# The newest queries' fetch moved ahead of the key store in a cross-attention kernel

## The chip, the cores and the metric

The kernel runs on one NeuronCore of a Trainium2 chip. The metric is the time of one execution in device microseconds. A core has a matrix engine (TensorE, "PE" in the profile), a vector engine (VectorE, "DVE"), a scalar engine (ScalarE, "ACT"), a general engine (GpSimd, "POOL") and SyncE ("SP"), which here does nothing but start transfers (DMAs). The engines run side by side. Each goes through its own list of instructions in order and stops where an instruction has to wait for another engine or for a transfer.

## What is computed

For each of 64 batch elements: 256 text rows of 512 numbers (x) and 256 audio rows of 384 numbers (the context), all in float32.

```
text_p  = x   @ W_text  + b_text        # queries before their layer norm
audio_p = ctx @ W_audio + b_audio       # keys before their layer norm; also the values
Q = layer_norm(text_p, g1, beta1)
K = layer_norm(audio_p, g2, beta2)
alpha = softmax(Q @ K.T / sqrt(512))
y = (alpha @ audio_p) @ W_out + b_out
out = layer_norm(y + x, g_out, beta_out)
```

## The kernel before

**What a batch element goes through.** TensorE contracts over the partition dimension, so what a product contracts over has to lie along the partitions. Rows come out of a projection with the hidden dimension along the free axis, but the scores need it along the partitions. The kernel turns them by way of DRAM. The normalised rows of the queries (`qr`) and of the keys (`kr`) are stored to a scratch tensor in DRAM (`qd`, `kd`; `Projection.store`, L425, one transfer of 512 KB) and fetched again as blocks of 32 by 32 (`qq`, `kq`; `Projection.fetch`, which calls `squares`, L88, four transfers of 128 KB). VectorE then transposes each block of 32 by 32 in place (`turn`: L91 for the queries, L446 for the keys), and ScalarE applies gain and shift per hidden column (`affine`, L453). The exponentials take the same way (`store_e` L556, `fetch_e`, tiles `ed` and `eq`), and x and the context are fetched as squares from the inputs (`load_x`, `load_c`, tiles `xq` and `cq`), and once more as plain rows (`load_x_rows` L112, `load_c_rows` L116).

**Products.** Each projection (queries, keys, output) is one matrix product of two by two blocks, written with seven block products instead of eight (`Blocks.products`, L482); VectorE adds them out of the accumulator banks into the rows (`Blocks.leave`, L494). Six banks (`p_pj`) serve all three projections in turn. Two more (`p_at`) take scores and context.

**Rounds.** The order on each engine is written out by hand. The main loop runs over b = 0 to 61. Round b does, in this order:

1. scores of element b, then the rest of the output of element b − 2; the squares of x and context of b + 3 are turned; row maxima and exponentials of b;
2. the query products of b + 2, between them the division of the exponentials;
3. SyncE: fetch of the queries and the keys of b + 1, store of the exponentials of b, load of context squares and x squares of b + 4, fetch of the exponentials of b, x rows of b, context rows of b + 1;
4. turn and affine of the queries of b + 1 (VectorE, ScalarE); context product of b − 1; turn and affine of the keys of b + 1; the output of b − 2 is settled and stored;
5. normalisation (`normalise`, L415) and store of the queries of b + 2;
6. the key products of b + 2, their evictions, normalisation and store;
7. most of the output products of b − 1.

So on SyncE's queue, in order, one round reads: q fetch (b + 1), k fetch (b + 1), e store, context squares, x squares, e fetch, x rows, context rows, output store, q store (b + 2), k store (b + 2). A fetch waits until its store has landed. A store waits until its rows are ready. All these transfers go through one hardware queue onto the core's 16 transfer engines.

The first round fetches nothing in step 3 (its own queries and keys are fetched ahead of the loop). Rounds 60 and 61 load no further squares. After the loop the last two elements are written out by hand; that part begins with the fetch of the queries and keys of element 63. Buffers: the squares `qq` and `kq` have two each, the scratch tensors `qd` and `kd` three each.

Of the kernel before, what the change touches and what calls it, by code (L numbers as in the profile page):

```python
# [22 lines left out]
def kernel(  # L23
# [43 lines left out]
    B, L, D = x.shape  # L67
# [28 lines left out]
    def load_c(b):  # L96
        cq = blk.tile([P, S // SQ, DA // NQ], F32, tag="cq", name=f"cq_{b}")
        squares(cq, c[b])
        blocks[b] = [cq]

    def load_x(b):
        xq = blk.tile([P, L // SQ, D // NQ], F32, tag="xq", name=f"xq_{b}")
        squares(xq, x[b])
        blocks[b].append(xq)
# [5 lines left out]
    def load_x_rows(b):  # L110
        x_rows[b] = xin.tile([P, LT, D], F32, tag="x", name=f"x_{b}")
        nc.sync.dma_start(x_rows[b], x[b].rearrange("(t p) d -> p t d", p=P))  # L112

    def load_c_rows(b):
        c_rows[b] = cin.tile([P, ST, DA], F32, tag="c", name=f"c_{b}")
        nc.sync.dma_start(c_rows[b], c[b].rearrange("(t p) d -> p t d", p=P))  # L116
# [16 lines left out]
    def row(v, name):  # L133
        t = const.tile([P, H], F32, tag=name, name=name)
        nc.sync.dma_start(t, v.rearrange("(o h) -> o h", o=1).broadcast_to([P, H]))
        return t
# [621 lines left out]
    def turn_next(b):  # L758
        xT[b] = turn_x(b)
        xs[b] = sum_x(xT.pop(b))  # L760
        cT[b] = turn_c(b)
        cs[b] = sum_c(cT.pop(b))
# [7 lines left out]
    q, k, xT, cT = {}, {}, {}, {}  # L770
# [111 lines left out]
    for b in range(B - 2):  # L882
        three = b + 3 < B
        at = Attention(b)
        at.scores()
        if done:
            done.o.leave(3, 4)
            done.o.leave(7)
            done.add_x()
        if three and b:  # L890
            turn_next(b + 3)
        if last:
            last.turn_e()
        at.maxima()
        at.exponentials()
        if not b:
            k[1].turn()
        q2 = q[b + 2] = Blocks("q", b + 2, xs.pop(b + 2), wt_blocks, bt_sb)
        q2.products(*((1, 6) if b else (1, 2, 6)))
        q2.leave(1)  # L900
        q2.leave(6)
        at.reciprocals()
        at.divide_e()
        if not b:
            k[1].affine(g2_sb, be2_sb)
        if b:
            q[b + 1].fetch()
            k[b + 1].fetch()
        at.store_e()
        if b + 4 < B:  # L910
            load_c(b + 4)
        if not b:
            at.fetch_e()
        if b + 4 < B:
            load_x(b + 4)
        if b:
            at.fetch_e()
            load_x_rows(b)
        if not three:
            load_x_rows(b + 1)  # L920
        load_c_rows(b + 1)
        if b == 1:
            go_sb = row(g_out, "go")
            beo_sb = row(beta_out, "beo")
        if done:
            done.statistics()
        q2.products(*((2, 5) if b else (5,)))
        q2.leave(2, 5)
        q2.products(3, 4)
        q2.leave(3, 4)  # L930
        q2.products(7)
        q2.leave(7)
        q2.square()
        q2.scales()
        q[b + 1].turn()
        if not b:
            turn_next(3)
        if done:
            done.shift(0)
            done.shift(1)  # L940
        if last:
            last.context()
        q[b + 1].affine(g1_sb, be1_sb)
        if b:
            k[b + 1].turn()
            k[b + 1].affine(g2_sb, be2_sb)
        if done:
            done.settle(0)
            done.settle(1)
            done.store()  # L950
        q2.normalise()
        q2.store()
        if last:
            last.start_products()
        k2 = k[b + 2] = Blocks("k", b + 2, cs.pop(b + 2), wa_blocks, ba_sb)
        k2.products(1, 6)
        k2.leave(1)
        k2.leave(6)
        k2.products(2, 5)
        k2.leave(2, 5)  # L960
        k2.products(3, 4)
        k2.leave(3, 4)
        k2.products(7)
        k2.leave(7)
        k2.square()
        k2.scales()
        k2.normalise()
        k2.store()
        if last:
            last.o.products(1, 6)  # L970
            last.o.leave(1)
            last.o.leave(6)
            last.o.products(2, 5)
            last.o.leave(2, 5)
            last.o.products(3, 4)
            last.o.products(7)
        done, last = last, at


    at = Attention(B - 2)  # L980
    q[B - 1].fetch()
    k[B - 1].fetch()
    load_x_rows(B - 1)
    load_c_rows(B - 1)
# [105 lines left out]
```

## Time and profile before

| | us |
|---|---|
| time, median of 3 runs | 1415.64 (1413.58 to 1415.87) |
| the profiled execution, whole | 1416.99 |
| its span | 1415.2 |
| TensorE busy | 1404.5 |
| VectorE busy | 1229.0 |
| ScalarE busy | 935.1 |
| GpSimd busy | 870.6 |
| share of the 16 transfer engines' time on the main queue | 80.0% |

The profile comes from one execution; the times come from runs of their own. A busy line such as "1404.5 (99%) x6437" gives busy time, share of the span and number of instructions. In a list of waits each line gives who waited at which line for whom, the total in us, how often, and the longest. A line of the view in order of time gives start and duration in us, engine, source line, operation, tile written and tile read; transfers are shown on SyncE's queue ("SPq") with the time that issuing them took, not the time they travelled. The page gives the latter separately as the median from issue to landing:

```profile
kq<-kd SPq DMA_DIRECT2D x256, 128.0 KB, 3.4
qd<-qr SPq DMA_DIRECT2D x64, 512.0 KB, 4.8
qq<-qd SPq DMA_DIRECT2D x256, 128.0 KB, 3.3
```

SyncE's own waits, the largest of them:

```profile
SPq L425 <- ACT kr L415: 197.0, 62, 3.2
SPq L425 <- DVE kr L494: 93.5, 61, 1.9
SPq L425 <- ACT qr L415: 68.4, 59, 1.4
SPq L556 <- ACT e L552: 68.0, 57, 1.4
...
SPq L88 <- DMA kd<-kr: 19.2, 58, 1.0
SPq L88 <- DMA qd<-qr: 17.1, 18, 4.6
```

### The profile page before, as it was taken

What the parts mean: (1) busy time and instruction counts of PE and PEld (TensorE: products, weight loads), DVE (VectorE), ACT (ScalarE), POOL (GpSimd) and SP (SyncE); (2) the same over time, 40 slices, a digit from 0 to 9 for tenths busy, and PEclk for the clock granted to TensorE, in tenths of its full rate; (3) what the DMA queues carried; (4) which work ended last, traced back from release to release, by engine and by line L of the source; (5) the groups of instructions that cost most, each with busy time, mean ns of one, the idle gap of its engine ahead of it and who ended that gap; (6) DMA issues with size and microseconds to landing.
All of it is one profiled execution on the core that took longest, in us unless ns stands there. A gap on an engine that the chain in (4) does not pass through costs nothing.

```text
span 1415.2 us, 22762 instructions
## 1 busy us (share of the span) xinstructions
PE 1404.5 (99%) x6437; PEld 1219.7 (86%) x6437; DVE 1229.0 (87%) x1757; ACT 935.1 (66%) x2298; POOL 870.6 (62%) x1294
## 2 busy tenths in 40 slices
PE   9999999999999999999999999999999999999998
PEld 5788888888888888888888888888888888888885
DVE  5789888988988988988889889889888898898887
ACT  4667676676676676766766766767667667667663
POOL 5557656656666666566566666665665665666645
PEclk9999999999999999999999999999999999999999
DMA  7898887887888787887887887877888788788864
GB/s 198 212 249 245 243 238 220 240 241 221 234 232 229 232 228 236 234 226 237 229 233 232 220 241 233 227 238 228 226 242 239 221 236 239 222 235 226 229 199 125
DMA packets 450579, 322.58 MB, mean 228 GB/s; under 512 B 154900, under 2 KB 382996, under 8 KB 450452
## 3 DMA queue, kind: packets, MB, share of 16 engines
q1 hardware_dynamic: 450356, 320.98, 80.0%
q8 instruction: 52, 0.85, 0.3%
q14 instruction: 75, 0.61, 0.1%
q10 hardware_dynamic: 96, 0.13, 0.0%
HBM read 204.09 MB, written 116.92 MB: 227 GB/s over the span
## 4 chain that ended last, share of the span: by engine, by line
PE 94%; DMA 3%; DVE 1%; POOL 1%; SPq 1%; ACT 0%; issue 0%; DVEq 0%; ACTq 0%
PE ps_q L482 26%; PE ps_k L482 20%; PE ps_y L482 20%; PE ps_sc L521 15%; PE ps_z L587 12%; DMA qd<-qr 1%; PE ps_y L634 1%; DMA ba<-in_L_xattn_b_audio_dram 1%; DMA qq<-qd 0%; DMA xq<-in_x_dram 0%; DMA bt<-in_L_xattn_b_text_dram 0%; SPq L88 0%; DMA c<-in_ctx_dram 0%; DVE qr L494 0%; DMA kd<-kr 0%
## 5 line engine op out<-in xcount | busy, mean ns | idle before, releaser
L494 DVE TENSOR_TENSOR qr<-ps_q,qr 128x512 f32<-128x512 f32 x252 | 174.3, 692 | 88.3 <-PE ps_q L482 85.3
L521 PE MATMUL ps_sc<-kT,qT 128*128 128x256 f32 x1024 | 231.7, 379 | 1.1 <-ACT qT L453 1.1
L348 POOL TENSOR_SCALAR ve<-var 128x2 f32<-128x2 f32 x126 | 43.1, 342 | 290.3 <-ACT junk L387 290.1
L521 PEld LDWEIGHTS ps_sc<-kT,qT 128*128 128x128 f32 x1024 | 194.2, 190 | 28.8 <-ACT qT L453 2.1
L538 ACT ACTIVATE e<-ps_sc,nmx 128x256 f32<-128x256 f32 x128 | 59.4, 469 | 228.7 <-DVE nmx L531 228.7
L603 POOL TENSOR_TENSOR yr<-yr,x 128x512 f32<-128x512 f32 x124 | 155.6, 1277 | 70.2 <-DVE yr L494 70.2
L482 PE MATMUL ps_q<-wtsum,xsum 128*128 128x256 f32 x756 | 193.8, 379 | 0.2 <-POOL xsum L312 0.2
L494 DVE TENSOR_TENSOR kr<-ps_k,kr 128x512 f32<-128x512 f32 x252 | 174.3, 692 | 22.1 <-DVE kr L494 0.5
L494 DVE TENSOR_TENSOR yr<-ps_y,yr 128x512 f32<-128x512 f32 x248 | 171.5, 692 | 21.8 <-DVE yr L494 0.5
L482 PE MATMUL ps_k<-wa,cT 128*128 128x256 f32 x630 | 177.1, 379 | 0.0
L587 PE MATMUL ps_z<-eT,c 128*128 128x256 f32 x768 | 176.2, 379 | 0.0
L482 PE MATMUL ps_y<-wao,zT 128*128 128x256 f32 x620 | 174.1, 379 | 0.0
L350 POOL TENSOR_TENSOR rstd<-ve,nhalf 128x2 f32<-128x2 f32 x192 | 157.1, 818 | 16.0
L587 PEld LDWEIGHTS ps_z<-eT,c 128*128 128x128 f32 x768 | 145.9, 190 | 20.3 <-issue 0.5
L482 PEld LDWEIGHTS ps_q<-wtsum,xsum 128*128 128x128 f32 x756 | 143.6, 190 | 20.0 <-POOL xsum L312 0.6
L453 ACT ACTIVATE qT<-qT,columns 128x256 f32<-128x256 f32 x256 | 132.9, 591 | 8.0 <-DVE qT L91 8.0
L482 PEld LDWEIGHTS ps_k<-wa,cT 128*128 128x128 f32 x630 | 119.6, 190 | 16.2
L453 ACT ACTIVATE kT<-kT,columns 128x256 f32<-128x256 f32 x256 | 132.0, 586 | 1.4 <-DVE kT L446 1.0
L415 ACT ACTIVATE kr<-kr,rstd 128x512 f32<-128x512 f32 x126 | 84.0, 714 | 72.3 <-POOL rstd L350 72.3
L482 PEld LDWEIGHTS ps_y<-wao,zT 128*128 128x128 f32 x620 | 117.7, 190 | 16.0
L387 ACT ACTIVATE junk<-kr 128x512 f32<-128x512 f32 x126 | 79.4, 630 | 77.5 <-DVE kr L494 73.1
L482 PE MATMUL ps_q<-wt,xT 128*128 128x256 f32 x504 | 129.1, 379 | 0.0
(159 smaller groups left out, 2973.0 us busy)
## 6 DMA issues: line engine op xcount, KB each, us to landing
kd<-kr SPq DMA_DIRECT2D x64, 512.0 KB, 3.1
kq<-kd SPq DMA_DIRECT2D x256, 128.0 KB, 3.4
qd<-qr SPq DMA_DIRECT2D x64, 512.0 KB, 4.8
qq<-qd SPq DMA_DIRECT2D x256, 128.0 KB, 3.3
xq<-in_x_dram SPq DMA_DIRECT2D x252, 128.0 KB, 2.8
x<-in_x_dram SPq DMA_DIRECT2D x63, 512.0 KB, 4.2
out_dram<-yr SPq DMA_DIRECT2D x62, 512.0 KB, 4.8
cq<-in_ctx_dram SPq DMA_DIRECT2D x252, 96.0 KB, 2.4
```

Of the source, the lines that this page charges most:

```text
L348: nc.gpsimd.tensor_scalar(ve, var, EPS, None, ALU.add)
L350: nc.gpsimd.tensor_tensor(r, ve, nhalf[:, :n], ALU.pow)
L387: nc.scalar.activation(junk, self.rows[:, t, :], AF.Square, scale=1.0 / math.sqrt(H), accum_out=self.var[:, t : t + 1],)
L415: nc.scalar.mul(row, row, self.r[t])
L453: nc.scalar.activation(self.T[:, k, :], self.T[:, k, :], AF.Identity, bias=bet[:, k : k + 1], scale=gam[:, k : k + 1],)
L482: nc.tensor.matmul(place, lhsT=side, rhs=w, start=(i == 0), stop=(i == len(pairs) - 1))
L494: add = lambda o, i0, i1: nc.vector.tensor_tensor(o, i0, i1, ALU.add)
L521: nc.tensor.matmul(self.sc[:, t, :], lhsT=self.qT[:, k, bass.ts(t, P)], rhs=self.kT[:, k, :], start=(k == 0), stop=(k == HC - 1),)
L538: nc.scalar.activation(self.e[:, t, :], self.sc[:, t, :], AF.Exp, bias=self.nmx[:, t : t + 1], accum_out=self.den[:, t : t + 1],)
L587: nc.tensor.matmul(ps[:, j, :], lhsT=self.c_sb[:, s, bass.ts(lo + j, P)], rhs=self.eT[:, s, :], start=(s == 0), stop=(s == ST - 1),)
L603: nc.gpsimd.tensor_tensor(self.y[:, t, :], self.y[:, t, :], x_rows[self.b][:, t, :], ALU.add)
L634: nc.tensor.matmul(ps, lhsT=self.zT[:, k, bass.ts(t, P)], rhs=wao_sb[:, k, :], start=(k == 0), stop=(k == AC - 1),)
```

## The change

The fetch of the newest queries moves from step 3 of the following round to step 6 of the round that made them, between the normalisation of the keys and the store of the keys. The fetch ahead of the hand-written end goes away, since round 61 has then done it.

```
         if not b:
             k[1].affine(g2_sb, be2_sb)
         if b:
-            q[b + 1].fetch()
             k[b + 1].fetch()
         at.store_e()
...
         k2.square()
         k2.scales()
         k2.normalise()
+        q2.fetch()
         k2.store()
         if last:
             last.o.products(1, 6)
...
     at = Attention(B - 2)
-    q[B - 1].fetch()
     k[B - 1].fetch()
     load_x_rows(B - 1)
     load_c_rows(B - 1)
```

On SyncE's queue one round then reads: k fetch (b + 1), e store, context squares, x squares, e fetch, x rows, context rows, output store, q store (b + 2), q fetch (b + 2), k store (b + 2). The order of instructions on the other engines is the same.

More of the change, by code (lines that the diff above doesn't have):

```diff
@@ L906 @@
         if b:
-            q[b + 1].fetch()
             k[b + 1].fetch()
@@ L967 @@
         k2.normalise()
+        q2.fetch()
         k2.store()
@@ L980 @@
     at = Attention(B - 2)
-    q[B - 1].fetch()
     k[B - 1].fetch()
```

## The prediction

> **What bounds the kernel now.** I read the engine rows of the page first, then TensorE's list of waits, then SyncE's instructions in order of time in one middle round, then the same in the first rounds, where SyncE is late.
>
> ```profile
> PE 1404.5 (99%) x6437; PEld 1219.7 (86%) x6437; DVE 1229.0 (87%) x1757; ACT 935.1 (66%) x2298; POOL 870.6 (62%) x1294
> ```
> ```profile
> PE ps_ones L195 <- POOL ones L123: 1.5, 1, 1.5
> PE ps_sc L521 <- ACT qT L453: 1.1, 1, 1.1
> PE ps_q L369 <- DMA wt<-in_L_xattn_W_text_dram: 0.5, 1, 0.5
> ```
> TensorE sets the time. Its longest waits happen once each, all in the first 61 us; none recurs in the rounds. A round takes 21.58 us (the q store is issued at 704.22 and next at 725.81). So nothing can be gained in a round; a round can only become longer. The question is whether something else now needs more than 21.58 us for a round. The candidate is SyncE (SP), through which every transfer goes in order:
>
> ```profile
> 704.22 0.37 SPq L425 DMA_DIRECT2D qd<-qr  x1
> 709.38 0.36 SPq L425 DMA_DIRECT2D kd<-kr  x1
> 709.83 2.40 SPq L88 DMA_DIRECT2D qq<-qd  x4
> 712.52 1.78 SPq L88 DMA_DIRECT2D kq<-kd  x4
> 715.79 0.38 SPq L556 DMA_DIRECT2D ed<-e  x1
> 716.21 1.98 SPq L88 DMA_DIRECT2D cq<-in_ctx_dram  x4
> 718.24 1.93 SPq L88 DMA_DIRECT2D xq<-in_x_dram  x4
> 720.21 1.93 SPq L88 DMA_DIRECT2D eq<-ed  x4
> 722.24 0.40 SPq L112 DMA_DIRECT2D x<-in_x_dram  x1
> 722.73 0.41 SPq L116 DMA_DIRECT2D c<-in_ctx_dram  x1
> ```
> The columns are start, time on the queue, line and transfer. SP waits 4.8 us ahead of the key store (704.59 to 709.38, for ScalarE's kr), then issues the q fetch while the key store travels, then the k fetch. In that pause the q store travels too, and this is what the round's picture hides:
>
> ```profile
> 89.82 1.80 SPq L88 DMA_DIRECT2D qq<-qd  x4
> 91.73 1.88 SPq L88 DMA_DIRECT2D kq<-kd  x4
> ...
> 100.20 0.46 SPq L112 DMA_DIRECT2D x<-in_x_dram  x1
> ...
> 108.85 1.80 SPq L88 DMA_DIRECT2D qq<-qd  x4
> 110.75 1.87 SPq L88 DMA_DIRECT2D kq<-kd  x4
> ...
> 120.78 0.40 SPq L112 DMA_DIRECT2D x<-in_x_dram  x1
> ...
> 128.75 2.00 SPq L88 DMA_DIRECT2D qq<-qd  x4
> ```
> Here SP runs behind and is held by nothing but itself and its transfers, since the q fetch waits for the q store to land. So this is its free loop: 108.85 − 89.82 = 19.03 us, and 19.90 us for the next (one e store took 1.99 us instead of 0.38). Against 21.58 us SP has 1.7 to 2.5 us a round to spare, and by the fourth round it has caught up. Any wait that the change adds to this loop is free up to that amount and is paid in every round beyond it.
>
> **The change, part by part.** Nothing is added to any engine: the four q fetch issues (128 KB each) move from after the key store to before it, for queries one round newer. TensorE, VectorE, ScalarE and GpSimd keep their order. The q buffer that the early fetch fills was last read by the query turn a round earlier, so it adds no wait. For the queries themselves all gets earlier, and nobody gains: VectorE's turn of qq waits for its transfer 4 times in the whole run, 9.0 us in sum, none of it in the settled rounds.
>
> What is new is one wait. The q fetch reads what the q store wrote, so SP now stands until the q store has landed, and behind it stands the key store. In the records of single transfers, over the 55 settled rounds, the q store's last data packet ends at 4.3 us (mean; 3.3 to 5.2 for eight rounds in ten) on the round's clock where the key store is issued at 4.87. The q store is slow to land because 512 KB of x, 384 KB of c and 512 KB of output are ahead of it. From the last packet to the waiting SP instruction it takes 0.43 us (the key store's packets end at 7.62, its k fetch starts at 8.05). So the q fetch starts near 4.75, right where the pause ends: the pause is already spent on the landing and hides none of the fetch.
>
> Second, the k fetch waits for the key store. Before, the q fetch (2.4 us of issue) lay under the key store's trip:
>
> ```profile
> kd<-kr SPq DMA_DIRECT2D x64, 512.0 KB, 3.1
> ```
> Now SP has nothing to do on that trip. The cost, from the start of the q fetch (Q) to that of the k fetch: before, in the free loop, 1.90 us (the two 91.73 − 89.82 and 110.75 − 108.85). After: four issues 1.90 us, then the key store, then its landing. Lower bound: 3.1 us as in the row, so Q + 1.9 + 3.1 + 0.1 = 5.1. Upper bound: it also queues behind the q fetch. That fetch's packets begin 1.0 us after its issue (as the key store's do, 4.87 to 5.88); q and k fetch together take 4.9 us of packets, so one takes 2.45; the key store's packets then take 1.75 and the notice 0.43: Q + 1.0 + 2.45 + 1.75 + 0.43 = 5.63. I take 5.6, as all go through one queue and in the trace its packets come in order of issue.
>
> The free loop after, piece by piece:
> 1. x issue to q fetch (x, c, output, q store through a full queue, and the notice): 108.85 − 100.20 = 8.65 and 128.75 − 120.78 = 7.97; mean 8.3.
> 2. q fetch to k fetch: 5.6 (5.1 to 5.6).
> 3. k fetch to the next x issue. Clean: 100.20 − 91.73 = 8.47; the middle round gives 722.24 − 712.52 − 1.5 (its e store waits for ScalarE) = 8.25. Over the 55 rounds the issues run longer now and then (16 have x more than 0.6 us late): k fetch 1.87 + gap 0.1 + e store to x 6.84 = 8.8 on average. Today such delays vanish in the slack; in a loop without slack each counts. I take 8.8.
>
> Sum 8.3 + 5.6 + 8.8 = 22.7 us; the lowest of each gives 7.97 + 5.1 + 8.25 = 21.3, the highest 8.65 + 5.63 + 8.8 = 23.1. As a check, with 1.9 in place of 5.6 the sum is 19.0, against the 19.03 and 19.90 seen. So the loop is longer than TensorE's 21.58 by some 1.1 us; I use 22.65, +1.07 a round.
>
> How TensorE feels it. Late k squares hold VectorE's key turn, and in order behind it stand the two output settles, then the evictions of the key products:
> ```profile
> 720.71 1.30 DVE L446 STREAM_TRANSPOSE kT<-kq 128x512 f32<-128x512 f32 x2
> ```
> Key products and output products share six banks. VectorE's first key evictions start at 702.34 and give the first bank back at 703.7; TensorE's third output group, which needs it, starts at 705.8: about 2.1 us of lateness are free. In the first full round the k fetch moves from 91.73 to about 96.9 (1.5 us inherited from the round before, where it goes from 71.57 to about 73.1, and 3.7 from this one); its squares land some 3.9 us later (1.0 + 2.45 + 0.43), at 100.8, against a key turn at 96.88. So 3.9 − 2.1 = 1.8 us are lost there already, and the slack of the start is gone. From then on 58 rounds (the last two load no further squares, and SP catches up) lose 1.07 each: 62 us. Sum: 1.8 + 62 = 64 on the profiled run's 1416.99 (span 1415.2, 1.8 us around it; the median 1415.64 is 1.4 lower). That gives 1481 against the profiled run and 1479.6 against the median: **1480 us**, +4.5%.
>
> A rule speaks against the change: the Trainium skill, "DMA: Bandwidth & Descriptors", section "Rules for kernel authors", says to issue a transfer early and wait on its semaphore late, and its section "Anatomy of one DMA" says that such waits happen on the issuing sequencer and that a DMA has about 2.0 us of fixed cost, mostly the receipt. Here the row gives 3.1 − 1.75 = 1.35 us. As an estimate by the page, the added trip would be 0.65 us longer and the loop 23.3 us: 1518 us.
>
> The stalls are about 1 us in 21.6, and the granted clock is 1.00 in every stretch but the last 16 us (0.89, TensorE busy 8.35 of 16); I leave it at 1.00. The skill's "TensorE: Matmul & The Clock Gate", Part 1, halves the clock only after about 3.4 us idle, which would change nothing in the sum.
>
> **Rivals.**
> A. *The pause does hide it* (no change, 1416 us). The loop must stay under 21.58, 1.1 us less than my sum. For it: the lowest bounds give 21.3, and the transfer engines stand still in the old pause:
> ```profile
> 729.30:730.90 1.60, 1.60 (x9) 1.39 (x8) 1.39 (x3) 1.31 (x2) 0.46 (x2) 1.00 0.00 0
> ```
> (the last two numbers are share and GB/s), which the q fetch could fill. Against: another idle gap opens after the key store, and the free loop reproduces 19.0 to 19.9. Chance 0.12.
> B. *The loop is worse*, from 23.3 us: behind late key turns the settles, q stores and output stores come late too, so that the q store's landing slips beyond the SP chain. From the k fetch: squares landed 3.9, key turn to q store 5.1 (720.71 to 725.81) is 9.0, while SP reaches the q store at 8.8 + 1.5 = 10.3. So it decides only if ScalarE or VectorE lose 1.3 us more. With +1.8 a round: 1417 + 4 + 104 = 1525 us. Chance 0.13.
> C. *Faster*, since queries are there a round sooner: the only wait on queries in a round's place is the 1.1 us ahead of the scores, and it belongs to queries whose fetch isn't moved. Ceiling 1415.6 − 1.1 = 1414.5, which is within 0.2% (2.8 us, about what a measurement of this kernel can tell from no change). The chance of more is 0.02.
>
> **How the numbers follow.** Forecast (loop between 21.7 and 23.3) 0.73, A 0.12, B 0.13, C 0.02. A loop of 21.9 gives 1417 + 1 + 58 × 0.32 = 1437, one of 23.1 gives 1417 + 3 + 58 × 1.52 = 1508. I set the range at 1428 to 1515, which leaves out A, C and most of B. Slower by over 0.2%: 0.86; within: 0.12; faster: 0.02.
>
> **What would show it.** In SP's order of time: q fetch within 0.5 us of the q store's landing, k store 2 us behind it, k fetch 3.1 to 3.7 us behind that; SP's wait on the key store grows from 19.2 us in all to about 200; its waits on ScalarE's kr (197.0 us) and e (68.0 us) all but vanish; VectorE's key turn waits for kq in most rounds; TensorE's round is 22.6 us. I am wrong if rounds stay at 21.58 with the k fetch stable on the round's clock (then piece 1 or 2 is too long), or if TensorE waits with SP idle (then B).

## The result, and the profile after

The changed kernel takes 1489.2 us (median of 6 runs, 1486.45 to 1498.28), the kernel before 1415.76 us beside it. The ratio is 1.0528, 95% interval 1.0509 to 1.0548: 73 us slower. The forecast was 1480 us, in a range from 1428 to 1515.

First the engine rows and the chain of work that ended last, from the page of the changed kernel, and below them that chain from the page of the kernel before:

```profile
PE 1422.8 (96%) x6437; PEld 1219.5 (82%) x6437; DVE 1193.8 (80%) x1757; ACT 936.3 (63%) x2298; POOL 818.3 (55%) x1294
...
DMA 32%; DVE 23%; SPq 22%; PE 10%; ACT 6%; issue 6%; DVEq 1%; POOL 0%; ACTq 0%
```
```profile
PE 94%; DMA 3%; DVE 1%; POOL 1%; SPq 1%; ACT 0%; issue 0%; DVEq 0%; ACTq 0%
```

Before, TensorE made up 94% of that chain. Now it makes up 10%, and transfers and SyncE's queue together 54%. The instruction counts are the same as before. TensorE is the most occupied engine still, at 96%, and yet it no longer sets the time.

SyncE in order of time, the same stretch as was shown of before (start, time on the queue, line, transfer):

```profile
703.16 1.80 SPq L88 DMA_DIRECT2D qq<-qd  x4
705.07 0.39 SPq L425 DMA_DIRECT2D kd<-kr  x1
709.86 1.78 SPq L88 DMA_DIRECT2D kq<-kd  x4
711.75 0.40 SPq L556 DMA_DIRECT2D ed<-e  x1
712.19 2.01 SPq L88 DMA_DIRECT2D cq<-in_ctx_dram  x4
714.24 1.93 SPq L88 DMA_DIRECT2D xq<-in_x_dram  x4
716.21 1.93 SPq L88 DMA_DIRECT2D eq<-ed  x4
718.24 0.40 SPq L112 DMA_DIRECT2D x<-in_x_dram  x1
718.73 0.41 SPq L116 DMA_DIRECT2D c<-in_ctx_dram  x1
719.24 0.42 SPq L743 DMA_DIRECT2D out_dram<-yr  x1
719.75 0.42 SPq L425 DMA_DIRECT2D qd<-qr  x1
726.25 1.80 SPq L88 DMA_DIRECT2D qq<-qd  x4
728.16 0.39 SPq L425 DMA_DIRECT2D kd<-kr  x1
731.40 1.78 SPq L88 DMA_DIRECT2D kq<-kd  x4
```

There are only two holes left in the queue: from the q store (ends 720.17) to the q fetch (726.25), and from the key store (ends 705.46, 728.55) to the k fetch (709.86, 731.40). Both are a store on its way, with the fetch of the same rows waiting for it. Everything else is issued back to back. SyncE's list of waits says the same for the whole run (the first of the two key store trips shown is a long one; over the 64 waits the mean is 3.0 us):

```profile
SPq L88 <- DMA qd<-qr: 398.5, 64, 8.0
SPq L88 <- DMA kd<-kr: 192.3, 64, 4.9
```

The waits on ScalarE that led that list before are gone: 197.0 us for the keys of the rounds became none, the row of 68.0 us for the exponentials became 0.3. SyncE is hardly held by the engines any more; it holds them. VectorE and TensorE, from their lists:

```profile
DVE kT L446 <- DMA kq<-kd: 162.2, 60, 4.0
DVE qT L91 <- DMA qq<-qd: 32.0, 34, 1.7
```

and VectorE's row for the keys in the kernel before:

```profile
DVE kT L446 <- DMA kq<-kd: 2.3, 4, 1.1
```

TensorE's, after the change:

```profile
PE ps_y L482 <- DVE kr L494: 51.6, 45, 2.1
```

VectorE stands at the key turn in 60 rounds, 2.7 us each time, and TensorE then waits for a bank that VectorE's late key evictions give back late. These waits hold 51.6 of the 69.5 us by which the profiled span grew (1415.2 to 1484.7). TensorE's busy time, whose matmul ends are modelled, grew by 18.3 us with the same instructions, which is about the rest.

### The profile page after: what moved, and what is told of

It is laid out like the page before. It is cut to its first block, busy times and chain, and to the rows that moved or that the text cites. A ratio compares the mean times of both kernels' runs of the same rounds, so it can differ in the third digit from the quotient of the medians.

```text
span 1484.7 us, 22760 instructions
## 1 busy us (share of the span) xinstructions
PE 1422.8 (96%) x6437; PEld 1219.5 (82%) x6437; DVE 1193.8 (80%) x1757; ACT 936.3 (63%) x2298; POOL 818.3 (55%) x1294
## 4 chain that ended last, share of the span: by engine, by line
DMA 32%; DVE 23%; SPq 22%; PE 10%; ACT 6%; issue 6%; DVEq 1%; POOL 0%; ACTq 0%
SPq L88 20%; DMA c<-in_ctx_dram 13%; DMA kd<-kr 11%; DVE qr L494 4%; DMA kq<-kd 4%; DVE xT L91 4%; DVE kr L494 3%; DMA qd<-qr 3%; DVE cT L91 3%; PE ps_q L482 3%; DVE nmx L531 2%; DVE eT L91 2%; ACT e L552 2%; DVE yr L733 2%; PE ps_y L482 2%
## 5 line engine op out<-in xcount | busy, mean ns | idle before, releaser
L348 POOL TENSOR_SCALAR ve<-var 128x2 f32<-128x2 f32 x126 | 35.7, 284 | 438.4 <-ACT junk L387 435.8
L446 DVE STREAM_TRANSPOSE kT<-kq 128x512 f32<-128x512 f32 x124 | 80.9, 690 | 162.2 <-DMA kq<-kd 162.2
```

The costliest lines, as they stand in the source:

```text
L446: nc.vector.transpose(self.T.rearrange("p k (q t j) -> p t q k j", t=self.nt, j=SQ)[:, t], self.sq[:, t * NQ : (t + 1) * NQ].rearrange("p ...
```

## The experiments

Eleven kernels, each timed in rounds against the kernel before. "After" in a diff is the changed kernel. The theory to be tested: SyncE's round is a loop (q store, landing, q fetch, key store, landing, k fetch, loads, next q store) that now takes longer than TensorE's 21.58 us. The rivals: the place in the program, the sum of bytes, VectorE's order, or only one of the two waits.

| kernel | median, us | ratio to before, 95% interval |
|---|---|---|
| e1, two lines swapped back | 1415.4 | 0.9991 to 1.0010 |
| e2, row loads into the new wait | 1419.1 | 1.0017 to 1.0036 |
| e3, k fetch behind e store and context squares | 1486.3 | 1.0487 to 1.0519 |
| e4, key turn later | 1474.0 | 1.0395 to 1.0429 |
| e5, q store ahead of the output store | 1422.0 | 1.0024 to 1.0051 |
| e6, after with an extra load | 1515.7 | 1.0684 to 1.0719 |
| e7, before with the same load | 1416.8 | 0.9999 to 1.0018 |
| e8, context squares into the new wait | 1420.5 | 1.0020 to 1.0041 |
| e9, key store started by ScalarE | 1813.3 | 1.2788 to 1.2830 |
| e10, before with q fetch behind k fetch | 1456.6 | 1.0275 to 1.0309 |
| e11, before with the landing wait alone | 1418.7 | 1.0010 to 1.0029 |

**e1: the order or the place?**

```
         k2.normalise()
-        q2.fetch()
         k2.store()
+        q2.fetch()
```

> The two lines of the new place are swapped: key store first, then the fetch of the newest queries, still in the round that made them. SyncE's order of transfers is then that of the kernel before. Loop theory (SyncE's own loop, q store -> landing -> q fetch -> key store -> landing -> k fetch -> loads, is longer than TensorE's 21.58 us): the loop falls back to 19 to 20 us, the time to 1416 us (+-3). Rival (fetching a round sooner is itself the cost, through the buffer or the place in the program): stays near 1489 us.

It came out at 1415.4 us. Fetching the queries "a round sooner" costs nothing; the order of two neighbours on SyncE costs 73 us.

**e6 and e7: a dose of 0.5 us on SyncE, in either kernel.** `extra` is one load of 64 KB from x.

```
         at.store_e()
+        if b:
+            extra(b)
         if b + 4 < B:
```

> The changed kernel with one extra load of 64 KB from x into an unused tile behind the e store in rounds 1 to 61 (extra work, read by nobody). Loop theory: about 0.5 us more on SyncE (an issue of such a transfer takes 0.48 us), paid in each of some 59 rounds: +28 us, 1510 to 1525 us. Rival (another engine or the sum of waits elsewhere sets the round): no change, 1489 us.

> The kernel before with the same extra load of 64 KB. Loop theory: the loop grows from 19 to 20 us by 0.5 us and stays below 21.58: no change, 1416 us (+-3). Rival (SyncE or the transfers are at their limit before the change too): +10 us or more.

The same load adds 26.5 us to the changed kernel (1515.7 − 1489.2), which is 0.45 us for each of 59 rounds, and 0.9 us to the kernel before, whose interval holds no change. In e6 SyncE's loop goes from 22.74 to 23.17 us, and the piece it was put into grows from 8.55 to 9.04. So SyncE's time is paid nearly in full after the change, and hardly at all before. This is the plainest evidence that the bound has moved.

**e11: the landing wait alone.** The fetch stays late, but a small read of the stored new queries (`touch`, 64 KB) stands ahead of the key store.

```
         k2.normalise()
+        touch(q2.d)
         k2.store()
```

> The kernel before with one small extra fetch (64 KB) of the queries just stored, into an unused tile, ahead of the key store. SyncE then waits for the q store's landing in front of the key store as in the changed kernel, but the whole q fetch still lies over the key store's trip. Loop theory: x issue to the small fetch 8.7, its issue and the key store 0.5, the key store's landing 3.1, then 8.55: loop 20.8 us, below 21.58, the key store 0.4 us later than before: 1416 to 1422 us. Rival (the wait for the q store's landing alone is the cost): above 1450 us.

1418.7 us, 0.2% above before. SyncE's waits in front of the key store (in this kernel the fetch of `touch` is L110 and the store L431):

```profile
SPq L110 <- DMA qd<-qr: 320.4, 62, 7.7
SPq L431 <- ACT kr L421: 7.9, 12, 1.8
```

SyncE waits for the q store's landing in 62 rounds, and this hardly costs anything: the new wait takes the place of the old one for the keys (197.0 us became 7.9), and the q fetch still covers the key store's trip.

**e8 and e3: the landing wait with the key store's trip covered again.** In e3 the cover was the e store and the context squares:

```
-        if b:
-            k[b + 1].fetch()
         at.store_e()
         if b + 4 < B:
             load_c(b + 4)
+        if b:
+            k[b + 1].fetch()
```

> The changed kernel with the k fetch behind the e store and the context squares' load, which then cover the key store's trip; the q fetch stays where the change put it. Loop theory: 2.5 us of the 3.6 us from key store to k fetch are covered, loop 22.7 - 2.5 = 20.2 us; the k fetch is then held by ScalarE's e, comes near 13.7 on the round's clock and its squares about 1.5 us behind the key turn's old place, less than the 2.1 us that are free: 1416 to 1425 us. Rival (the wait for the q store's landing in front of the key store is alone the cost): that wait is untouched, 1470 us or more.

The expectation failed: 1486.3 us. But not because the trip's cover doesn't matter. SyncE's waits in e3:

```profile
SPq L88 <- DMA qd<-qr: 287.2, 64, 6.8
SPq L556 <- ACT e L552: 201.3, 61, 5.0
...
SPq L88 <- DMA kd<-kr: 4.0, 3, 2.9
```

The key store's trip is covered (4.0 us in place of 192.3), and SyncE now waits 3.3 us a round for ScalarE's exponentials. The k fetch hangs on those, and the chain in order of time for that round shows where it goes on:

```profile
704.60 0.92 ACT e L552 x2
705.54 0.38 SPq L556
...
709.65 3.42 DMA kq<-kd
...
713.79 0.67 DVE kT L446
714.46 1.29 DVE yr L733 x2
715.76 0.61 DVE kr L494
```

Exponentials, e store, k fetch, landing, VectorE's key turn, and then all of VectorE's evictions up to the next row maxima, from which the next exponentials follow. This is a second loop, through VectorE, and it happens to take 22.8 us too. By the expectation's own numbers the k squares would land some 4.0 us behind the start of their fetch; the last of them landed 4.8 us behind it (708.23 to 713.08). VectorE, which had been free since 709.33, stood 3.8 us at the key turn, where the expectation allowed for a lateness of 1.5. So e3 does not answer its question. e8 asks it again without ScalarE in it:

```
+        if b + 4 < B:
+            load_c(b + 4)
         if b:
             k[b + 1].fetch()
         at.store_e()
-        if b + 4 < B:
-            load_c(b + 4)
```

> The changed kernel with the load of the context squares (four issues, 384 KB, no wait on any engine) between key store and k fetch; the e store comes behind the k fetch as it was. It asks the question of e3_kfetch_later without hanging the k fetch on ScalarE's e. Loop theory: 2.05 us of issue move into the 3.6 us between key store and k fetch, loop 22.7 - 2.05 = 20.7 us, the k squares land at most 0.8 us later: 1416 to 1425 us. Rival (the cover of the key store's trip doesn't matter, only the wait in front of the key store does): 1470 us or more.

1420.5 us. SyncE's wait for the key store falls from 192.3 to 40.3 us, and all but 5 us of the loss go with it.

**e2 and e5: shortening the other half, the way to the q store's landing.** e2 moves the row loads from behind the e fetch into the wait between key store and k fetch:

```
         if b:
+            load_x_rows(b)
+            if not three:
+                load_x_rows(b + 1)
+            load_c_rows(b + 1)
             k[b + 1].fetch()
...
             at.fetch_e()
-            load_x_rows(b)
-        if not three:
-            load_x_rows(b + 1)
-        load_c_rows(b + 1)
+        if not b:
+            load_c_rows(b + 1)
```

> The changed kernel with the x rows and context rows (896 KB, two issues) moved from behind the e fetch to between key store and k fetch, into SyncE's new wait; the bytes of a round stay the same. Loop theory: 1.0 us of issue and 2.4 to 3.5 us of transfers leave the piece ahead of the q fetch and lie in the 3.3 us wait instead; the loop falls from 22.7 to 18.5 to 20 us, below 21.58, and the time to 1416 to 1425 us. Rival (the transfer engines as a whole are the limit, so the sum of bytes decides): stays within 1% of 1489 us.

e5 exchanges output store and q store:

```
             done.settle(1)
-            done.store()
         q2.normalise()
         q2.store()
+        if done:
+            done.store()
```

> The changed kernel with the q store ahead of the output store: 512 KB less are in front of the q store in the queue, and the output travels while SyncE waits. Loop theory: 1.3 us of transfer and 0.4 us of issue leave the piece from x issue to q fetch, loop 22.7 - 1.5 = 21.2 us, just below TensorE's 21.58; with the uneven rounds 1416 to 1430 us. Rival (the q store's landing is not on the loop, only the key store's trip is): stays near 1489 us.

1419.1 and 1422.0 us. Neither changes the bytes of a round, so the sum of bytes is not the limit. e2 in SyncE's order of time:

```profile
704.51 0.39 SPq L743 DMA_DIRECT2D out_dram<-yr  x1
706.30 0.38 SPq L425 DMA_DIRECT2D qd<-qr  x1
709.13 1.80 SPq L88 DMA_DIRECT2D qq<-qd  x4
711.45 0.38 SPq L425 DMA_DIRECT2D kd<-kr  x1
711.94 0.58 SPq L112 DMA_DIRECT2D x<-in_x_dram  x1
712.63 0.69 SPq L116 DMA_DIRECT2D c<-in_ctx_dram  x1
715.36 1.99 SPq L88 DMA_DIRECT2D kq<-kd  x4
```

The q store now lands in 2.8 us, as only the output is ahead of it, and SyncE again has time to wait ahead of the output store and the q store (702.63 to 704.51, 704.90 to 706.30). In e5 the piece from the x issue to the q fetch goes from 8.67 to 7.32 us, by the 1.3 us of the output's 512 KB.

In e2, e5 and e8 what is lost is lost at the start. Set against the profiled run of the kernel before, TensorE's score products of the 14th round start 2.1, 5.0 and 4.0 us late, and those of the 62nd round just as late; from the 14th on every round takes 21.58 us. So in the settled rounds all three are bound by TensorE again. In the changed kernel the same lateness goes on growing to 67.8 us.

**e4: VectorE's order.** Key turn and key affine go behind the settles and the q store.

```
-        if b:
-            k[b + 1].turn()
-            k[b + 1].affine(g2_sb, be2_sb)
         if done:
             done.settle(0)
             done.settle(1)
             done.store()
         q2.normalise()
         q2.store()
+        if b:
+            k[b + 1].turn()
+            k[b + 1].affine(g2_sb, be2_sb)
```

> The changed kernel with VectorE's key turn and ScalarE's key affine behind the two output settles and behind the query normalisation, so that output store and q store no longer stand behind a late key turn. Loop theory: SyncE hardly waits for either of them (12 and 2 us in the whole run), so the loop stays 22.7 us and the time 1480 to 1495 us. Rival (VectorE's in-order wait for kq is the cause): VectorE loses its 162 us of waiting there and the time falls below 1450 us.

1474.0 us: below the expected span, which began at 1480, and far from the rival's. VectorE's waits in e4:

```profile
DVE qT L91 <- DMA qq<-qd: 105.9, 62, 3.6
DVE kT L446 <- DMA kq<-kd: 54.5, 60, 3.7
```

They moved from the key turn to the query turn of the next round: 160 us in all against 194. So VectorE's waiting was not taken away here, and the rival is tested only in part; the dose of e6, which lengthens SyncE's queue and nothing of VectorE's work, is the better evidence against it. SyncE's loop is 22.55 us instead of 22.74, each of its pieces a little shorter. Over 58 rounds that is 11 us; the two profiled runs differ by 8.4 us (1478.04 and 1486.45), the medians by 15. Why the pieces are shorter was not settled.

**e10: the uncovered trip alone.** The kernel before, with key store, k fetch, q fetch in that order:

```
         if b:
-            q[b + 1].fetch()
             k[b + 1].fetch()
+            q[b + 1].fetch()
```

> The kernel before with the q fetch and the k fetch of a round swapped: key store, k fetch, q fetch. The key store's trip is then uncovered as in the changed kernel, but nothing waits for the q store's landing in front of the key store. Loop theory: from x issue to the key store's landing about 8.2 + 1.75 = 10 us, then two fetches and the loads 1.9 + 8.55, loop 20.4 us, below 21.58: 1416 to 1425 us; the query squares land up to 1.5 us behind VectorE's old query turn, which is within what is free. Rival (the uncovered trip of the key store is alone the cost): above 1450 us.

Another clear miss, after e3: 1456.6 us. By its number alone the rival would have won. The lists of waits of SyncE and VectorE speak against that:

```profile
SPq L425 <- ACT kr L415: 198.1, 62, 3.2
SPq L88 <- DMA kd<-kr: 157.6, 64, 4.4
SPq L425 <- ACT qr L415: 88.0, 62, 1.6
```
```profile
DVE qT L91 <- DMA qq<-qd: 155.0, 63, 5.0
```

SyncE waits for ScalarE as long as in the kernel before (198.1 and 197.0 us): its own loop still has slack, as the theory has it. But the query squares are fetched 1.9 us behind the k fetch, and VectorE, whose query turn comes first, waits 2.5 us a round for them. From there the chain runs through VectorE's key evictions, ScalarE's normalisation and the key store back to the k fetch, again without TensorE. So it is a late fetch that costs here, as in e3, and not a full SyncE. The key store's trip lies on this loop as well: in the round shown by the chain it is 2.77 us, from 708.51 to 711.29. So e10 does not clear the uncovered trip; it shows that it can cost by another road than SyncE's loop. The expectation had taken VectorE's free time for granted.

**e9: the key store started by ScalarE.**

```
-            nc.sync.dma_start(self.d.rearrange("(t p) h -> p t h", p=P), self.rows)
+            queue = nc.scalar if self.name == "k" else nc.sync
+            queue.dma_start(self.d.rearrange("(t p) h -> p t h", p=P), self.rows)
```

> The changed kernel with the key store started by ScalarE, right behind the normalisation that it does itself, and not by SyncE; the q fetch stays where the change put it. The key store then no longer stands behind SyncE's wait for the q store's landing. Loop theory: from q fetch to k fetch SyncE needs its four issues and what is left of the key store's trip, the transfers of the key store may lie in front of the q fetch instead (up to 1.75 us): loop 20 to 21.4 us, 1416 to 1430 us. Rival (the early q fetch costs by its transfers, which meet the key store's): stays above 1470 us.

1813.3 us, the largest miss. SyncE in order of time:

```profile
704.03 11.92 SPq L88 DMA_DIRECT2D eq<-ed  x4
716.04 0.40 SPq L112 DMA_DIRECT2D x<-in_x_dram  x1
```

The four fetches of the exponentials take 11.92 us instead of 1.93; the fourth starts at 715.64, just after a key store that ScalarE started at 711.97 has landed. Its list of waits has the key store with 562.8 us in 62 waits. The fetch does not use those keys. The trace tells why. Each transfer reports its landing on one of eight semaphores (210 transfers on each), which serve both queues, and most issues wait for the semaphore that they will themselves use, that is, for an earlier transfer. The key store issued at 711.97 reports on semaphore 107. The fourth fetch of the exponentials reports on 107 too, and waits for it first. One round later the two share semaphore 100 (740.51 and 743.32).

So this kernel says nothing on the theory: it has a new wait that the edit was not meant to have. What the key store would cost on another queue without it is open.

## Why the prediction was right, point by point

**TensorE bound before, nothing to gain.** Right: no variant is faster than before outside its interval.

**SyncE's free loop was 19 to 20 us, with slack.** Right: e7 adds 0.5 us to it and 0.9 us to the run.

**The pieces of the new loop**, means over the settled rounds of the changed kernel, in us:

| piece | predicted | measured |
|---|---|---|
| x issue to q fetch | 8.3 | 8.67 |
| q fetch to k fetch | 5.6 | 5.52 |
| k fetch to x issue | 8.8 | 8.55 |
| loop | 22.65 | 22.74 |

The choice of the upper bound for the second piece, with the key store queued behind the q fetch, was right: in the trace the key store's packets come behind those of the q fetch (from 706.23, where those end at 706.43). The uneven rounds do count, but by less than was booked: the third piece has 8.55 us, between the clean 8.25 to 8.47 and the 8.8 assumed. The first piece, from two early rounds, was 0.4 us too small. These two errors offset each other, so that the loop came out within 0.1 us is in part luck. The loop of 23.3 us that the prediction estimated from the Trainium skill ("DMA: Bandwidth & Descriptors", section "Anatomy of one DMA") lies 0.6 us above the measured one. That section is about transfers started by GpSimd, and these are started by SyncE; the bound worked out from the rows came nearer.

**The first rounds.** Near the mark, but by two errors that offset each other. The k fetch of the first two was put at 73.1 and 96.9; it came at 71.72 and 94.35. In the first, the key store was started at 68.40 as before, since the q store had landed by 66.48. So the k squares were less late than booked. But less lateness was free: the 2.1 us come from a settled round. In the first full round of the kernel before, VectorE's key evictions start at 99.51, which by the same 1.36 us gives the bank back at 100.9, only 0.6 us ahead of the third output group (101.47). In the changed kernel they start at 101.04, and TensorE stands for that bank:

```profile
102.59 1.10 PE L482 MATMUL ps_y<-wao,zsum 128*128 128x256 f32 x4 [2.13 <-DVE kr L494]
```

It had begun this round 1.2 us earlier than the kernel before (scores at 80.88 and 82.04) and begins the next 1.2 us later (104.83 and 103.62). So the loss is there, 1.2 us against the run before where 1.8 was booked.

**The sum.** 1.16 us a round (22.74 − 21.58) by 58 rounds is 67 us against 62 predicted. TensorE's own rounds say the same: its scores are 1.2 us late at 104.83 and 67.8 us late 58 rounds on (1423.22 against 1355.45). That is most of the 69.5 us between the two profiled spans (1484.7 − 1415.2). The profiled run is the shortest of the six; their spread up to 1498 us is not explained here and makes up the rest to the median's 73.

**How TensorE feels it.** Right: the key turn waits for kq in 60 rounds, and TensorE stands at the output products for a bank, at the third group as forecast.

**The clock.** The prediction left it at 1.00. In the rounds that holds but for three stretches of 3.4 us, from 467.7, 559.8 and 1263.0 us. The first of them (the last three numbers are clock, share and GB/s):

```profile
467.70:471.10 3.40, 3.40 (x10) 2.69 (x9) 3.05 (x6) 1.61 (x5) 0.64 (x2) 0.50 0.67 144
```

Each comes after a stall of 1.9 to 2.0 us at the output products; the longest stall of the run after its start is 2.13 us. So the clock was halved after less idle time than the 3.4 us that the prediction took from the Trainium skill ("TensorE: Matmul & The Clock Gate", Part 1). At half clock for 10.2 us in all, TensorE loses 5.1 us at most, of 69.5, and part of that is caught up: the rounds with these stretches are the longest three (25.42, 24.74, 24.99 us), and the next ones are shorter than the mean (21.68, 22.33, 22.01).

**The rivals.** A (the pause hides it) named the right condition, a loop under 21.58: e2, e5 and e8 each bring the loop there and land 0.3 to 0.4% above before, all of it lost in the first rounds. B (worse, through VectorE) did not come about in the changed kernel, but loops through VectorE do occur, if other ones than B's: e3 and e10 are bound by them, where a fetch was moved behind what VectorE needed next. C was excluded.

**Neither wait alone.** The prediction charged the loss to two waits in one loop. e11 has the first without the second (+0.2%), e8 the changed order with the second mostly covered (+0.3%). The second without the first, e10, is slower for another reason, so that corner is argued from its waits and not from its time.

## What to carry to other kernels

A queue that issues in order has a round time of its own. Sum it up from one landing to the next, with every store that is followed by a fetch of the same rows counted as a full trip, and compare it with the bound engine's round. Before moving a fetch into a queue's pause, ask what the pause is waiting out: here a store was still travelling in it, and the fetch had been the cover for the next store's trip. Where two fetches leave late, look up which one the in-order consumer needs first.

## What the runs showed of the hardware that was not expected

From a store's last data packet to the SyncE instruction that waits for it took 0.4 to 0.5 us (in the changed kernel 0.46 in the mean for the key store, 0.42 for the q store). From the issue of the key store to its first packet, with nothing ahead of it in the kernel before, it took 0.9 us (709.38 to 710.25 in the middle round); the prediction had 1.0. The wait is mostly the queue ahead: the same 512 KB q store had landed 6.1 us after its issue was over with x, context and output rows ahead of it (720.17 to 726.25), and 2.5 us after with the output alone (706.68 to 709.13 in e2).

In 16 of 55 settled rounds of the kernel before, SyncE reached the x issue more than 0.6 us late, because some group of four fetches took 0.7 to 1.4 us longer to issue. Before the change this never reached TensorE: its settled rounds all take 21.58 us.
